# Four loads of 256 columns for each broadcast row in a four-layer graph attention kernel

## Chip, core and metric

The kernel runs on one core of a Trainium2 chip. The metric is the device time of one execution in microseconds (us). The time before is 2668.85 us, the median of three runs (2665.5 to 2671.96). The kernel is compiled as one straight program of 132436 instructions (a general path stands behind a branch at its end and is not taken with these inputs).

## The reference, cut to what matters

Sixteen graphs of 1024 nodes with 256 features pass through four layers. Each layer normalises, applies a ReLU, and adds a graph attention to its input:

```python
h = jnp.maximum(_layernorm(x, axis=-1), 0.0)
x = x + attention(h, adj, W, a_src, a_dst)        # four layers, the third with bias, ReLU, skip and layer norm per head
# inside, for a head:
e   = leaky_relu(s_src[:, :, None] + s_dst[:, None, :], slope)   # 1024 x 1024 for a graph and a head
e   = where(adj == 0, -inf, e)
out = softmax(e, axis=-1) @ (h @ W)
```

The first three layers have four heads of 64 columns, the last has one head of 256. All values are float32.

## The kernel before, in words

A softmax numerator of a head is a product of factors, so that for each block of 128 source nodes (a *tile*) one VectorE instruction makes 128 x 1024 numerators `p` from three things: the row `r`, which holds one value for each of the 1024 destination nodes and is the same in all partitions; a factor `fac` for each source node; and the mask. TensorE then multiplies the numerators (as weights, in pieces of 128 x 64) with the values `v`, 65 columns wide, and sums over the eight tiles of a head. A head has eight tiles, a unit (one layer of one graph) four heads, and 48 units of that kind are worked through in the order `ORDER`; the fourth layers of the graphs run beside them.

The row `r` comes to all partitions in four steps, in `prepare`:

- TensorE turns the values, VectorE copies them into the tile `row`.
- Two DMAs of the sync queue (SP) write them to DRAM, tensor `line`.
- For each head one DMA of the sync queue reads the head's 1024 values back to all 128 partitions (a source whose partition step is 0) into the tile `over`: named `rows` for the layers with four heads, of which there is one buffer (`ROWS = 1`), and `rows_one` for the last layer, also one buffer.
- ScalarE copies `rows` into one of two wide PSUM banks, `r` (`spread_row`), from which VectorE reads for eight tiles. `last_layer` copies quarters of `rows_one` in the same way.

As there is one `rows` buffer, the next row's load waits until ScalarE has copied the one before. The function `taken` says so to the planner, and the DMA waits for ScalarE's semaphore.

The order of all instructions is settled when the program is built. A planner (class `Plan`) keeps a clock for each engine. Each job is a generator that yields the engine it wants next and the earliest time; the loop at the end takes the step with the earliest planned time `when`, and the instructions go out in that order, each into its engine's queue. `plan.spend` moves an engine's clock; `plan.cost` has the costs, 400 ns of SP for a DMA. The queue of SP holds, besides the row loads: the loads of `x_cur` (128 KB each, eight for a graph), the transposed loads `mask` from `near`, the stores of `y` to `out_dram`, and the writes of `line`. SP takes them strictly in order, and a DMA that must wait for a semaphore holds up all behind it. The masks' source `near` is filled by casting DMAs that GpSimd issues.

PE's instructions are fetched by DMA while the program runs: the profile lists these transfers as a queue of their own, of the kind "instruction".

In the profile nearly every instruction has line 515, the line of the planner's helper that passes on each call (517 in the changed kernel, where the piece loads have lines of their own). Groups are therefore told apart by their tiles.

Of the kernel before, what the change touches and what calls it, by code (L numbers as in the profile page):

```python
# [20 lines left out]
P = 128  # L21
# [400 lines left out]
SPREAD = 0  # L422
SOONER = 300.0
AT_ONCE = -(10**6)
ACT_STATS = (0,)
SETTLE = 83.0
SECOND = 4000.0
# [109 lines left out]
def fast_path(  # L537
# [21 lines left out]
    nc = tc.nc  # L559
    ctx.enter_context(tc.manual_schedule())  # L560
    plan = Plan()
    pe, act, dve, pool, sp = (
        plan.engine(e, name)
        for e, name in (
            (nc.tensor, "PE"),
            (nc.scalar, "ACT"),
            (nc.vector, "DVE"),
            (nc.gpsimd, "POOL"),
            (nc.sync, "SP"),
        )  # L570
    )
    G, N, F = x.shape
# [82 lines left out]
    def bank():  # L655
        k = min(free_banks(), key=lambda k: banks[k])
        banks[k] = None
        if k >= BANKS:
            spare[0] += 1
            return ps_o.tile([P, 512], F32, name="po"), k  # L660
        return ps_p.tile([P, 512], F32, name=f"pp{k}"), k

    def drop(k: int):
        banks[k] = plan.now
# [17 lines left out]
    def wide_bank(dt=F32):  # L682
        k = wide_free.index(min(t for t in wide_free if t is not None))
        wide_free[k] = None
        return ps_r.tile([P, 4096 // mybir.dt.size(dt)], dt, name=f"r{k}"), k

    def leave_wide(k: int):
        wide_free[k] = plan.now
# [3 lines left out]
    def weights(layer: int):  # L692
# [43 lines left out]
        for k in range(KC):  # L736
            for c in range(KC):
                to = c * KC + k
                pe.transpose(pw[:, to * P : (to + 1) * P], given[:, k, c * P : (c + 1) * P], ident)
        yield "ACT", None, AT_ONCE  # L740
        if n == 1:
# [4 lines left out]
        drop(at)  # L746
        yield "PE", free_bank, AT_ONCE + 1
        pa, at = bank()
        for k in range(KC):
            for half in range(0, P, P // 2):  # L750
                for c in range(KC):
# [6 lines left out]
                    )  # L758
        yield "ACT", None, AT_ONCE
        act.copy(wa[layer][:, :, :, w : w + 2], pa[:, : KC * 2 * n].rearrange("p (k h c) -> p k h c", k=KC, h=n))  # L760
# [116 lines left out]
    def normal(es: list, rs: bass.AP):  # L877
# [25 lines left out]
        for e in es:  # L903
            yield "ACT", None, AT_ONCE
            e.hT = work.tile([P, KC, 2 * P], F32, name="hT", bufs=PAIRS)
# [5 lines left out]
    def project(e, i: int):  # L911
# [16 lines left out]
        e.read = plan.now  # L928
        yield "ACT", None, AT_ONCE
        act.copy(u.v[:, 2 * e.pair + i, :width], pv[:, :width])  # L930
# [18 lines left out]
    def prepare(u: "Unit"):  # L949
# [3 lines left out]
        width = n * (w + 2)  # L953
        by_act = layer in ACT_STATS and u.g.b >= BY_ACT and (layer < 3 or u.g.b < G - 2)
        yield "ACT" if by_act else "DVE", lambda: (
# [14 lines left out]
        if by_act:  # L970
            for i in range(2 * NB):
# [6 lines left out]
                b, c = i % NB, i // NB  # L978
# [48 lines left out]
        turned(pm, mine[:, 1, :])  # L1027
        yield "DVE", None, AT_ONCE
        top = small.tile([P, 1], F32, name="top", bufs=3)
# [16 lines left out]
        c = small.tile([P, 4, MAXN], F32, name="c", bufs=2)  # L1046
# [35 lines left out]
        if direct:  # L1082
# [20 lines left out]
            else:  # L1103
                yield "DVE", None, AT_ONCE
                over = units.tile([P, N], F32, name="rows_one", bufs=1)
# [16 lines left out]
        flat = line[: n * NB]  # L1122
        for h in range(len(u.row), n):
            yield "SP", lambda: (u.before is None or len(u.before.ps) == u.before.many * NB) if n == 1 else taken(ROWS, 4 * u.turn + h)
            if n > 1:
                over = units.tile([P, N], F32, name="rows", bufs=ROWS)
            else:
                over = units.tile([P, N], F32, name="rows_one", bufs=1)
            sp.dma_start(over, bass.AP(tensor=flat.tensor, offset=flat.offset + h * N, ap=[[0, P], [1, N]]))
            u.row.append((over, plan.now))  # L1130
        if n == 1:
            add(u.until + LATE, last_layer(u), plan.now)

    def turned(to, of):

        for half in range(0, P, P // 2):
            pe.matmul(to[half : half + P // 2, : P // 2], of, ident[:, half : half + P // 2])

    def taken(count: int, k: int):

        k -= count
        return k < 0 or main[k // H].weighed > k % H
# [59 lines left out]
    def row_due():  # L1202

        if rowed[0] == len(main) * H or rowed[0] * NB - at_tile[0] > ROW_LEAD or not free_wide():
            return False
        u, h = main[rowed[0] // H], rowed[0] % H
        return len(u.row) > h and max(u.row[h][1], free_wide())

    def spread_row():

        u, h = main[rowed[0] // H], rowed[0] % H
        rowed[0] += 1
        r, k = wide_bank()
        act.copy(r, u.row[h][0])
        u.across[h] = r, k, plan.now
        u.weighed += 1
# [179 lines left out]
    def last_layer(u: "Unit"):  # L1396

        due = lambda: (
            u.ready
            and hasattr(u, "flat")  # L1400
            and at_tile[0] >= u.gate
            and not row_due()
            and (late[0] < LATE_TILES or (at_tile[0] == len(tiles) and room() is not None and late[0] < TILES - 1))
        )
        free = lambda: due() and free_wide() and max(u.g.loaded, u.ready, free_wide())
        soon = lambda: u.ready and at_tile[0] == len(tiles) and room() and late[0] < TILES - 1 and max(u.ready, room())
        begun = at_tile[0]
        part = N // u.many
        for i in range(u.many):
            if i == 1:  # L1410
                add(u.until + LATE_SUMS, last_sums(u), plan.now)
            for j in range(0, NB, u.many):
                if u.kept:
                    yield "DVE", soon
                    late[0] += 1
                    cover_late(u, i, j, u.kept[0][:, i * part : (i + 1) * part])
                    continue
                yield "ACT", free, begun + LATE + int((i * NB + j) * SPREAD)
                late[0] += 1
                r, at = wide_bank()  # L1420
                act.copy(r[:, :part], u.row[0][0][:, i * part : (i + 1) * part])
                yield "DVE", room, at_tile[0]
                cover_late(u, i, j, r[:, :part])
                leave_wide(at)
        if u.kept:
            leave_wide(u.kept[1])
# [157 lines left out]
    def add(until, gen, ready, first=None):  # L1584
        jobs.append([until, ready, *(first or next(gen))[:2], gen])
# [3 lines left out]
    while True:  # L1589
        while begins and (begins[0][0] <= at_tile[0] or not jobs):  # L1590
            _, gen, until = begins.pop(0)
            add(until, gen, 0.0)
        can = []

        def offer(engine, ready, until, what):
            can.append((max(plan.free[engine], ready), until, engine, what))

        if row_due():
            offer("ACT", row_due(), at_tile[0], "row")
        if at_tile[0] < len(tiles) and room() is not None:  # L1600
            u, h, j = tiles[at_tile[0]]
            if h in u.across and u.g.loaded and u.ready:
                offer("DVE", max(u.across[h][-1], u.g.at[j % NQ2], u.ready, room()), at_tile[0] + SLACK, "cover")
        first = reach()
        if first:
            offer("PE", first[0], at_tile[0] + SLACK, "gather")
        for job in jobs:
            ready = job[3] is None or job[3]()
            if ready:
                ready = max(job[1], ready)  # L1610
                engine = job[2]
                offer(engine, ready, job[0], job)
        if not can:
            assert not jobs and not begins and at_tile[0] == len(tiles), "nothing can go on"
            break
        best = {}
        for e in ("SP", "POOL", "DVE", "ACT", "PE"):
            mine = [c for c in can if c[2] == e]
            if mine:
                first = min(c[0] for c in mine)  # L1620
                best[e] = min((c for c in mine if c[0] <= first + NEAR), key=lambda c: c[1])
        when, _, engine, what = min(best.values(), key=lambda c: c[0])
        plan.now, plan.last = when, None
        if what == "row":
            spread_row()
        elif what == "cover":
            cover(*tiles[at_tile[0]])
            at_tile[0] += 1
        elif what == "gather":
            gather()  # L1630
        else:
            step = next(what[4], None)
            if step is None:
                jobs.remove(what)
            else:
                wait = 0.0 if step[0] == engine else MARGIN.get(step[0], 40.0) if at_tile[0] < len(tiles) else 40.0
                what[0] = step[2] if len(step) > 2 else what[0]
                what[1:4] = [(when if step[0] == engine else plan.now) + wait, *step[:2]]


    nc.vector.tensor_scalar(bad[:, 2:3], greatest[:, G * LAYERS - 1 :], 1.0 / LEAST, bad[:, 3:4], ALU.is_le, ALU.is_lt)  # L1641
# [47 lines left out]
```

## Time and profile before

| | before |
|---|---|
| median of three runs | 2668.85 us |
| the profiled execution's own time | 2667.53 us |
| its span, first to last instruction | 2665.8 us |
| granted TensorE clock | 0.997 |
| PE busy | 2578.2 us (97%) |
| VectorE (DVE) busy | 2342.0 us (88%) |
| GpSimd (POOL) busy | 1890.4 us (71%) |
| ScalarE (ACT) busy | 1272.3 us (48%) |
| DMA queue of the sync and scalar engines, share of 16 DMA engines | 20.7% |
| DMA queue of GpSimd | 10.3% |
| instruction queue q8 | 467 packets, 7.65 MB, 1.2% |
| row loads | 190 of `rows` and 13 of `rows_one`, 512 KB each |

The span is what the profiler sees between the first and the last instruction; 1.7 us of the execution's time lie outside it. PE means TensorE's matmuls and PEld its weight loads, which overlap them. "Idle before" is an engine's idle time just before an instruction, with what released it; "issue" means that nothing which the profile shows was waited for. SP has no busy time: its instructions only wait and issue.

### The profile page before, as it was taken

To read this page: it belongs to the slowest core of one execution; us is meant where nothing else is said; L and a number is where in the kernel's file an instruction comes from. 1 tells how busy PE (TensorE), PEld (TensorE's weight loads), DVE (VectorE), ACT (ScalarE), POOL (GpSimd) and SP (SyncE) were. 2 spreads that over 40 slices of the span, in tenths; PEclk is the share of its full clock that TensorE was granted. 3 is DMA by queue.
4 is the path that set the end of the run, shared out by engine and by line. 5 is a ranking of instruction groups with operands and counts; after the bars stand their busy time and mean duration, and the time that the engine had idled before them with its cause. 6 is when DMAs were issued, how large, how long until landed. Compare 5 with 4: busy or idle time off the path is not lost. (4 is left out here: it accounts for less than half of the span.)

```text
span 2665.8 us, 132436 instructions
## 1 busy us (share of the span) xinstructions
PE 2578.2 (97%) x59354; PEld 2207.9 (83%) x59354; DVE 2342.0 (88%) x3723; ACT 1272.3 (48%) x3378; POOL 1890.4 (71%) x3375
## 2 busy tenths in 40 slices
PE   9999999999999999999999999999999999899998
PEld 7888887787988788889888788988778798888775
DVE  6799998897999797889998897999888699998984
ACT  4633563654346456533564644356364553443441
POOL 5556888765778877747887875688787565977761
PEclk9999999999999999999999999999999999999999
DMA  8533233443132253313314441323334441111100
GB/s 133 84 75 73 59 69 69 76 87 71 64 66 63 63 85 82 76 57 77 72 55 82 88 72 59 83 50 75 74 74 79 83 85 57 53 47 55 40 23 32
DMA packets 211122, 184.44 MB, mean 69 GB/s; under 512 B 150640, under 2 KB 184560, under 8 KB 210544
## 3 DMA queue, kind: packets, MB, share of 16 engines
q1 hardware_dynamic: 143088, 159.10, 20.7%
q0 software_dynamic: 67456, 16.78, 10.3%
q8 instruction: 467, 7.65, 1.2%
q14 instruction: 111, 0.91, 0.1%
HBM read 191.77 MB, written 34.39 MB: 85 GB/s over the span
## 5 line engine op out<-in xcount | busy, mean ns | idle before, releaser
L515 DVE SCALAR_TENSOR_TENSOR p<-r,fac,mask 128x1024 f32<-128x1024 f32 (+2 forms) x2032 | 2075.7, 1079 | 159.8 <-PE pp L515 80.8
L515 PE MATMUL po<-v,p 128*64 128x65 f32 x32992 | 1060.9, 224 | 36.4 <-issue 15.8
L515 PEld LDWEIGHTS po<-v,p 128*64 128x64 f32 x32992 | 1021.5, 138 | 87.9 <-issue 30.8
L515 PEld LDWEIGHTS po<-v_flat,p 128*64 128x64 f32 x16384 | 507.8, 138 | 56.8 <-issue 24.4
L515 PE MATMUL po<-v_flat,p 128*64 128x65 f32 x16384 | 525.0, 223 | 29.4 <-issue 14.7
L515 PE MATMUL pp<-wa,hT 128*64 128x264 f32 (+1 forms) x4032 | 474.2, 385 | 0.1
L515 PE MATMUL pp<-v_one,p 128*64 128x257 f32 x3584 | 403.6, 380 | 3.2 <-ACT y L515 2.9
L515 PEld LDWEIGHTS pp<-wa,hT 128*64 128x64 f32 x4032 | 278.4, 137 | 132.1 <-ACT v L515 0.4
L515 PEld LDWEIGHTS pp<-v_one,p 128*64 128x64 f32 x3584 | 248.6, 136 | 128.0 <-ACT y L515 4.6
L515 POOL TENSOR_SCALAR hn<-x_cur,rs 128x256 f32<-128x256 f32 x504 | 274.6, 558 | 33.3 <-PE pp L515 29.3
L515 POOL TENSOR_TENSOR att<-att,inv 128x512 f32<-128x512 f32 x128 | 133.7, 1045 | 221.2 <-DVE inv L515 207.7
L515 ACT COPY att<-po 128x260 f32<-128x260 f32 x256 | 96.2, 376 | 377.1 <-PE po L515 353.1
L515 ACT COPY v<-pp 128x264 f32<-128x264 f32 (+1 forms) x392 | 148.5, 379 | 215.0 <-PE pp L515 213.8
L515 POOL TENSOR_TENSOR x_cur<-att,x_cur 128x512 f32<-128x512 f32 x190 | 225.8, 1188 | 14.9
L515 ACT COPY r<-rows 128x1024 f32<-128x1024 f32 x190 | 194.0, 1021 | 21.8 <-DVE p L515 15.5
L515 ACT ACTIVATE att<-att,s 128x64 f32<-128x64 f32 x512 | 190.9, 439 | 23.3 <-POOL s L515 23.0
L515 ACT ACTIVATE hT<-pp 128x512 f32<-128x512 f32 x250 | 136.4, 598 | 128.1 <-PE pp L515 127.4
L515 ACT ACTIVATE att<-po,inv 128x64 f32<-128x64 f32 x512 | 118.7, 321 | 145.6 <-DVE inv L515 143.6
L515 POOL TENSOR_TENSOR y<-y,x_cur 128x256 f32<-128x256 f32 x116 | 84.3, 732 | 131.6 <-ACT y L515 112.1
L515 POOL TENSOR_TENSOR v<-v,fac 128x512 f32<-128x512 f32 x131 | 136.2, 1064 | 11.5 <-ACT fac L515 11.4
L515 DVE BATCH_NORM_STATS2 st<-x_cur 128x6 f32<-128x256 f32 x400 | 138.3, 411 | 3.3 <-DMA x_cur<-in_x_dram 2.9
L515 PE MATMUL pp<-ident,hn 128*128 128x128 f32 x1000 | 137.0, 280 | 0.2 <-DVE row L515 0.2
(124 smaller groups left out, 2150.0 us busy)
## 6 DMA issues: line engine op xcount, KB each, us to landing
rows<-line SPq DMA_DIRECT2D x190, 512.0 KB
out_dram<-y SPq DMA_DIRECT2D x128, 128.0 KB
x_cur<-in_x_dram SPq DMA_DIRECT2D x112, 128.0 KB
near<-in_adj_dram POOLq DMA_DIRECT2D x112, 128.0 KB, 4.3
rows_one<-line SPq DMA_DIRECT2D x13, 512.0 KB
x_cur<-in_x_dram SPq DMA_DIRECT2D x4, 512.0 KB
line<-row SPq DMA_DIRECT2D x96, 8.0 KB
block<-in_adj_dram POOLq DMA_DIRECT2D x4, 256.0 KB, 10.4
```

What stands on the lines that cost most here:

```text
L515: r = call(*a, **k)
```

## The change

The load of a row becomes `PIECES = 4` loads of 256 columns each. The first is issued where the whole load stood. The other three go into a list, `pieces`, each with the SP clock of that moment. One of them is issued after each later planner step of SP, if it was in the list before that step; a piece whose time is more than `ROW_APART` = 2500 ns of planned time before the next step of any engine is issued at once; and before ScalarE's copy of a row all that are left are issued. The planner's clock is charged once, for the whole row as before, and the pieces are issued past the planner. So the order of the instructions on PE, DVE, ACT and POOL is the same in both kernels, and only the sync queue differs: 203 loads become 812.

```diff
+PIECES = 4
+ROW_APART = 2500.0
...
@@ prepare
                 over = units.tile([P, N], F32, name="rows_one", bufs=1)
-            sp.dma_start(over, bass.AP(tensor=flat.tensor, offset=flat.offset + h * N, ap=[[0, P], [1, N]]))
+            of = lambda c, size: bass.AP(
+                tensor=flat.tensor, offset=flat.offset + h * N + c, ap=[[0, P], [1, size]]
+            )
+            plan.spend("SP", *plan.cost("SP", "dma_start", (over, of(0, N)), {}), [flat.tensor.name])
+            size = N // PIECES
+            nc.sync.dma_start(over[:, :size], of(0, size))
+            for c in range(size, N, size):
+                pieces.append((plan.free["SP"], over[:, c : c + size], of(c, size)))
             u.row.append((over, plan.now))
...
+    pieces = []
+    def next_piece():
+        nc.sync.dma_start(*pieces.pop(0)[1:])
+    def all_pieces():
+        while pieces:
+            next_piece()
...
@@ spread_row, and the same in last_layer
         r, k = wide_bank()
+        all_pieces()
         act.copy(r, u.row[h][0])
...
@@ the planner's loop
         when, _, engine, what = min(best.values(), key=lambda c: c[0])
         plan.now, plan.last = when, None
+        while pieces and pieces[0][0] + ROW_APART < when:
+            next_piece()
+        waiting = len(pieces)
         if what == "row":
             spread_row()
...
+        if engine == "SP" and waiting:
+            next_piece()
```

In the built program 175 of the 203 rows have their four loads directly behind one another in the sync queue. In 28 something stands between them: a row of the other kind (8), a store of `y` (8), a load of `x_cur` (11), and three mask transposes (the row issued at 64.8 us).

More of the change, by code (lines that the diff above doesn't have):

```diff
@@ L1420, in last_layer @@
                 r, at = wide_bank()
+                all_pieces()
                 act.copy(r[:, :part], u.row[0][0][:, i * part : (i + 1) * part])
```

## The prediction

> **What bounds the kernel now.** I read the busy times first, then what PE waits for, then the moments of those waits in the timeline and the DMA window.
>
> ```profile
> PE 2578.2 (97%) x59354; PEld 2207.9 (83%) x59354; DVE 2342.0 (88%) x3723; ACT 1272.3 (48%) x3378; POOL 1890.4 (71%) x3375
> ```
>
> PE is the bound. Its idle time is 2665.8 - 2578.2 = 87.6 us, and a change that adds or removes no work of PE can win at most that. The waits of PE, longest total first (us in total, times, longest):
>
> ```profile
> PE po L515 <- issue: 30.5, 32, 2.6
> PE po L515 <- ACT att L515: 15.8, 16, 1.4
> PE po L515 <- DVE p L515: 9.4, 9, 2.7
> ```
>
> The largest is "issue": PE waits for nothing that the profile shows. With two more of 0.5 us there are 34 such waits, 30.9 us. The view of all waits has what the row loads hold up directly:
>
> ```profile
> DVE p L515 <- ACT r L515: 32.7, 8, 10.4
> ...
> ACT r L515 <- DMA rows<-line: 3.1, 2, 2.1
> ```
>
> ScalarE waits for a row's landing twice, 3.1 us in all. So a row that lands earlier wins nothing; the question is what the loads do to other traffic. The timeline from 1056 to 1066 us shows one "issue" wait:
>
> ```profile
> 1055.78 7.27 PE L515 MATMUL po<-v,p 128*64 128x65 f32 x241
> 1058.73 7.60 SPq L515 DMA_DIRECT2D rows<-line  x2
> 1064.30 1.92 PE L515 MATMUL po<-v,p 128*64 128x65 f32 x56 [1.24 <-issue]
> ```
>
> and the DMA window 1059 to 1064 us (40 slices of 0.125 us, busy tenths) shows what the DMA engines did:
>
> ```profile
> DMA  0000062897799999032424160000000000000000
> ...
> q1 hardware_dynamic: 144, 0.52, 32.2%
> q8 instruction: 1, 0.02, 1.2%
> ```
>
> A row load, issued at 1058.73, moves packets from 1059.70 to 1062.12 us. The one instruction packet of this window begins at 1061.98, when the row is nearly through, and takes 0.93 us; PE starts again at 1064.30. Nothing else moves after the row, and PE starves for 1.24 us. I read this as a fetch that stood behind the row's packets.
>
> The packet records of the trace bear it out. Each of the 34 waits ends 2.2 to 2.9 us after an instruction packet began. In 17 of them (16.6 us) a row load was moving when that packet began, or had ended within 0.5 us before. In 8 (9.5 us) a row load stood shortly before or after it, mixed with GpSimd's adjacency packets. In 9 (4.8 us) there was no row load.
>
> How late a fetch begins can be read too. I count PE's instructions at each fetch's start, and take the 15th percentile of its 21 neighbours as punctual. The 90 fetches that fall due while a row load moves begin 1.31 us late on the mean, and 35 of them over 1.5 us late. The 228 due with no other traffic: 0.46 us, 17. The 22 due while packets of 1024 bytes move (`x_cur` and `out_dram`: 128 KB per load, the size and shape of the new pieces): 0.44 us, 3.
>
> **The change part by part.**
>
> *Packet work.* A row is now 128 packets of 4096 bytes, 199 ns each on the mean. The four pieces make 512 packets of 1024 bytes, which in the `x_cur` and `out_dram` transfers take 49 ns: 4 x 49 = 196 ns. The load on the DMA engines stays the same. Per engine a whole row is a run of 8 x 199 = 1.6 us; a piece is 8 x 49 = 0.39 us.
>
> *Fetches.* The nearest row for four loads in a train is the eight loads of `x_cur` in the queue of SP:
>
> ```profile
> 727.53 0.34 SPq L515 DMA_DIRECT2D rows<-line  x1
> 727.91 3.97 SPq L515 DMA_DIRECT2D x_cur<-in_x_dram  x8
> ```
>
> Their last packet lands at 735.05 us. After the row ahead of them has drained they take 4.95 us, 0.62 us a load, and need the engines for 0.39 us of it. A train of pieces thus leaves gaps in which a fetch can start. If late starts fall from 35 of 90 to the rate of the 1024-byte loads, 3 of 22, the share (35/90 - 3/22)/(35/90) = 0.65 of the starvation goes. On the 17 clear waits that is 16.6 x 0.65 = 10.8 us; on the 8 mixed ones, where adjacency packets (unchanged, lateness 1.08 us) do part, I take half the share: 9.5 x 0.33 = 3.1 us. Sum 13.9 us. The ends are 0 and 26.1 us (all 25 waits gone).
>
> *What is late next.* PE then meets its other waits sooner, for `att` (15.8 us) and `p` (9.4 us) above all. DVE is busy for 88% of the span, so it can follow a faster PE nearly everywhere. I let four fifths through, an estimate from that 88% rounded down: 13.9 x 0.8 = 11.1 us.
>
> [...]
>
> *Issue and landing.* SP issues 609 loads more. A follower starts 0.37 us (`x_cur` behind `rows`) to 0.475 us (`x_cur` behind `x_cur`) after the one before: 225 to 290 us of SP, spread over queues that mostly stand and wait. For a row the last piece is issued 1.1 to 1.4 us later than the whole load was. The whole load lands 3.44 us after its issue (median), its first packet at 0.97 us. Four pieces at the train's 0.62 us land at 0.97 + 4 x 0.62 = 3.45 us: no change, and I take that. From below, by issue and packets alone, it is 1.1 + 0.97 + 0.39 = 2.5 us, sooner; from above 3.44 + 1.1 = 4.5 us. The copies of `rows` have a median of 6.2 us between landing and start, and 10 of 190 have under 1.5 us. 1.1 us more would move those ten copies by 7.4 us in total (less a 0.4 us semaphore floor, the smallest distance seen). The copy then waits for four semaphores instead of one; they are long met for the rest, and ACT is busy for 48% only.
>
> *Between the pieces.* A store or an `x_cur` load between pieces (19 rows) costs one or two issues, under 1 us in nearly all, and these copies have 2.8 us or more to spare: nothing. The eight rows whose trains mix with the other kind cost 0.4 us where 0.8 is left: nothing. One row, issued at 64.8 us, has three mask transposes between its pieces; its copy starts 0.38 us after landing, and the third transpose starts 4.3 us after the row. Its last piece lands about 3 us later than now, in the warm-up. I charge 1 us of it, with ends 0 and 3.
>
> [...]
>
> **The sum.** 11.1 - 1.0 = 10.1 us less. The profiled execution has 2667.53 us, so it gives 2657.4; the median is 1.3 us above that execution, so I predict 2668.85 - 10.1 = 2658.8, rounded to 2659 us.
>
> **Rivals.**
>
> *The fetch still waits, so nothing moves.* 175 of 203 rows have their four pieces directly behind one another, so the change mostly does not put them "behind the next instruction". If a fetch must wait for all that stands in an engine's queue, four pieces are the same 1.6 us as one row, and the starvation stays. For it: the same bytes follow each other at 0.37 us, as fast as an engine needs for a piece (0.39 us). Against it: the 22 fetches among the 1024-byte loads. Time: 2668.85 less at most 2 us, 2668.
>
> *Rows land late, slower.* If the pieces' landing slips by more than 1.5 us (slow descriptor making, four semaphores, SP's queue), the ten tight copies are late, then VectorE's tiles (its wait for `r` grows from 32.7 us), then PE. It decides from a slip of about 2 us: the sum over the copies is then 17.2 us against 7.4 at 1.1 us, and half of it, with fetches unchanged, gives 2668.85 + 8.6 = 2677 us. For it: the eight `x_cur` loads behind a row land up to 4 us after their last issue. Against it: a good part of that is the row ahead in the same queue, and twelve tile buffers stand between VectorE and PE.
>
> *All row-linked starvation goes.* 2668.85 - 26.1 = 2643 us, if PE loses nothing of it elsewhere.
>
> **How the numbers follow.** The forecast with its upper rival gets 0.68, nothing moves 0.17, late rows 0.15. A measurement of this kernel can tell about 0.2%, 5.3 us, from no change. Of the forecast's 0.68 I put 0.04 within that bound, since 3 late starts of 22 is a thin base; of the second case's 0.17, 0.11 within it and 0.03 on each side. So faster 0.67, same 0.15, slower 0.18. The range reaches from 2646 (most of the 26 us) to 2673 (into late rows, half a per cent above the forecast); about one in ten is left out on each side. The forecast's own range is 2646 to 2665.
>
> **What would show it.** Right: PE's "issue" waits fall from 30.5 us to between 14 and 20; q8 still has 467 packets; q1 has about 78000 packets more at the same share, 20 to 21%; ScalarE's wait for row DMAs stays under 6 us; PE's busy time stays within 3 us of 2578. Wrong: "issue" waits of 25 us or more (the fetch waits for the whole train), or "ACT r <- DMA rows" of tens of us with the wait of `p` for `r` grown (late rows).

## The result and the profile after

The changed kernel is slower. Its median is 2681.47 us (2675.66 to 2688.42, nine runs) against 2667.55 us (2662.92 to 2671.96, nine runs) of the kernel before on the same chips; the ratio is 1.0053, 95% interval 1.0043 to 1.0063. The prediction was 2659 us, faster.

The page of the profiled execution (2681.47 us, its span 2679.7):

```profile
span 2679.7 us, 133512 instructions
...
PE 2588.9 (97%) x59354; PEld 2217.1 (83%) x59354; DVE 2343.1 (87%) x3723; ACT 1271.5 (47%) x3378; POOL 1885.8 (70%) x3375
...
q1 hardware_dynamic: 230784, 159.14, 23.1%
...
q8 instruction: 467, 7.65, 1.1%
```

The span is 13.9 us longer. PE still bounds the kernel, and both parts of its time grew: idle time from 87.6 to 2679.7 - 2588.9 = 90.8 us, busy time by 10.7 us for the same 59354 matmuls. The packets rose by 87696 (77952 of data and 16 more of 4 bytes for each of the 609 further loads), the bytes by next to nothing, and the share of the queue went from 20.7% to 23.1%. What PE waited for:

```profile
PE po L517 <- issue: 35.5, 49, 2.0
PE po L517 <- ACT att L517: 17.3, 17, 3.1
PE po L517 <- DVE p L517: 10.1, 11, 2.7
```

"Issue" was to fall to between 14 and 20 us. It rose from 31.0 us in 34 waits to 35.5 in 49. From the view of all waits, the two lines on the row's own path:

```profile
DVE p L517 <- ACT r L517: 39.6, 9, 10.4
...
ACT r L517 <- DMA rows<-line: 24.2, 16, 9.6
```

ScalarE waited for rows eight times as long as before (3.1 us). So both signs that the prediction named for "wrong" are there, and the experiments had to say which of them costs.

The DMA window from 1066 to 1072 us shows one row in its four pieces (40 slices of 0.15 us):

```profile
DMA  0000000822244677669444432354544443214000
...
rows<-line SPq DMA_DIRECT2D x4, 128.0 KB
```

The whole row of the prediction's window took 2.4 us from its first packet to its last. The packets of this one run from 1067.19 to 1071.54 us, 4.35 us, with the engines mostly at a third to two thirds, and the next instruction packet begins at 1071.54. Over all rows with no other transfer of the sync queue near them, the last packet comes 4.74 us after the first issue (median of 93), before it was 3.36 us (81). A row keeps each engine 1.83 us instead of 1.53.

About half of PE's further busy time, 5.1 of 10.7 us by the estimate below, came through its clock. The profile's windows around one long "issue" wait (columns: stretch, length, busy time and instructions of PE, PEld, DVE, ACT and POOL, granted clock, DMA share, GB/s):

```profile
975.20:978.60 3.40, 1.35 (x46) 1.22 (x44) 3.40 (x5) 3.21 (x13) 3.40 (x5) 1.00 0.25 72
978.60:982.00 3.40, 3.40 (x71) 3.40 (x68) 1.70 (x2) 0.60 (x2) 3.10 (x5) 0.50 0.91 143
```

After a stretch of 3.4 us in which PE was busy for only 1.35 us, the clock is half for the next 3.4 us. The kernel before has three such stretches up to 2640 us, the changed one six. Half of the three further ones is an estimate of what they cost: 3 x 3.4 / 2 = 5.1 us. One of the three more is chance: it follows a wait of 2.77 us for `p` (ending at 2602.2 us) that the kernel before has too (at 2587.8 us), without half clock behind it. With the 3.2 us of idle time that is 8.3 of the 13.9 us; the other 5.6 us are busy time that no view explains (pauses too short to be listed as waits would look so, but that is not shown).

The warm-up has its own piece. The timeline of SP from 63 to 82 us (start, duration, line, what is issued):

```profile
63.95 0.34 SPq L1136 DMA_DIRECT2D rows<-line  x1
64.47 1.19 SPq L517 DMA_TRANSPOSE mask<-near  x1
65.70 0.58 SPq L1147 DMA_DIRECT2D rows<-line  x1
66.33 2.55 SPq L517 DMA_TRANSPOSE mask<-near  x1
...
70.75 0.58 SPq L1147 DMA_DIRECT2D rows<-line  x1
```

And of the timeline of all engines there the copy of this row and the matmuls that waited:

```profile
77.42 1.02 ACT L517 COPY r<-rows 128x1024 f32<-128x1024 f32 x1 [9.60 <-DMA rows<-line]
...
81.06 2.22 PE L517 MATMUL po<-v,p 128*64 128x65 f32 x36 [3.10 <-ACT att L517]
```

The last piece of the third row is issued 6.8 us after the first. The copy starts at 77.42 us, before it was 69.21, PE then stands for 3.1 us, and its clock is half from 80.9 us for 3.4 us. Between 60 and 90 us of the span the changed kernel falls 4.2 us further behind.

### The profile page after: what moved, and what is told of

Read it like the earlier page. It is cut to its first block, busy times and chain, and to the rows that moved or that the text cites. A ratio compares the mean times of both kernels' runs of the same rounds, so it can differ in the third digit from the quotient of the medians.

```text
span 2679.7 us, 133512 instructions
## 1 busy us (share of the span) xinstructions
PE 2588.9 (97%) x59354; PEld 2217.1 (83%) x59354; DVE 2343.1 (87%) x3723; ACT 1271.5 (47%) x3378; POOL 1885.8 (70%) x3375
## 3 DMA queue, kind: packets, MB, share of 16 engines
q1 hardware_dynamic: 230784, 159.14, 23.1%
## 5 line engine op out<-in xcount | busy, mean ns | idle before, releaser
L517 ACT COPY r<-rows 128x1024 f32<-128x1024 f32 x190 | 194.0, 1021 | 39.8 <-DMA rows<-line 24.2
```

The costliest lines, as they stand in the source:

```text
L517: r = call(*a, **k)
```

## The experiments

All are built on the kernel before unless said otherwise. But for the one named below, PE, DVE, ACT and POOL have the same instructions in the same order as before. "Issue" is PE's issue waits, "row wait" ScalarE's wait for row loads of both kinds, "late" the fetches (of 458) that begin over 1.5 us late, counted as in the prediction (how "punctual" is taken moves these by a few). The last three are read from one execution each, which can lie off the median: 2675.96 us for "64 columns, gap, 960 columns" with a median of 2681.63, 2695.25 for "8 x 16 partitions" with 2686.99.

| row load | ratio to before | 95% interval | issue us | row wait us | late |
|---|---|---|---|---|---|
| before: one load | 1 | | 31.0 | 3.9 | 87 |
| changed: 4 x 256 columns, spread | 1.0053 | 1.0043 to 1.0063 | 35.5 | 24.2 | 118 |
| 4 x 256 columns together | 1.0038 | 1.0025 to 1.0051 | 38.4 | 18.4 | 109 |
| 2 x 512 columns together | 1.0025 | 1.0011 to 1.0039 | 29.6 | 7.3 | 101 |
| 2 x 512 columns with a gap | 0.9996 | 0.9987 to 1.0005 | 27.0 | 7.1 | 91 |
| 64 columns, gap, 960 columns | 1.0052 | 1.0039 to 1.0064 | 36.9 | 14.7 | 116 |
| one load, and 512 bytes to 128 partitions | 1.0040 | 1.0027 to 1.0053 | 38.4 | 5.1 | 114 |
| 16 partitions, gap, 112 partitions | 0.9988 | 0.9976 to 1.0000 | 24.0 | 16.3 | 87 |
| 2 x 64 partitions | 0.9998 | 0.9989 to 1.0006 | 27.4 | 16.3 | 93 |
| 2 x 64 partitions with a gap | 0.9983 | 0.9972 to 0.9993 | 20.5 | 21.5 | 84 |
| 4 x 32 partitions together | 0.9932 | 0.9918 to 0.9946 | 15.7 | 15.6 | 54 |
| 4 x 32 partitions, spread as in the change | 0.9949 | 0.9936 to 0.9962 | 12.5 | 17.6 | 53 |
| 8 x 16 partitions | 1.0076 | 1.0059 to 1.0094 | 11.4 | 92.0 | 59 |
| one load in bfloat16 | 0.9950 | 0.9937 to 0.9964 | 18.2 | 1.9 | 77 |

**Column pieces, nothing between them.** In `prepare`, in place of the one load (`of` and the planner's charge as in the change):

```diff
+            for c in range(0, N, N // 4):
+                nc.sync.dma_start(over[:, c : c + N // 4], of(c, N // 4))
```

> The four column loads of each row stand directly behind one another in the sync queue, none behind another instruction. Theory A (the train of four loads keeps the DMA engines longer than one load, 3.8 us against 2.4 us from its first to its last packet, so that more instruction fetches start late and PE starves): as slow as the changed kernel, 2677 to 2686 us, PE's issue waits 34 to 40 us. Theory B (rows land about 1.4 us later, the copies wait, then VectorE, then PE): also 2677 to 2686. Theory C (what stands between the pieces of 28 rows, the three transposes in the warm-up above all, is the cost): back to 2666 to 2671 us.

2678.58 us, and 38.4 us of issue waits. So theory C, what stands between the pieces, is not the main cost. The two intervals, 1.0025 to 1.0051 here and 1.0043 to 1.0063 for the change, overlap; but this kernel gains no lag worth naming between 60 and 90 us (0.5 us against 4.2), so some of what lies between them is the row in the warm-up.

**The row late, its bytes together.** A load of 64 columns, two loads of one value into another tile `late_to`, then 960 columns:

```diff
+            nc.sync.dma_start(over[:, :64], of(0, 64))
+            for c in range(2):
+                nc.sync.dma_start(late_to[:1, c : c + 1], <one value of line>)
+            nc.sync.dma_start(over[:, 64:], of(64, N - 64))
```

> Each row in a load of 64 columns, two single values to another place, and then one load of 960 columns: the large load starts about 1.1 us later than in the kernel before, as the last piece does, but its packets stay large and together. Theory A: the time from first to last large packet stays at 2.4 us, so 2667 to 2672 us and issue waits near 31 us. Theory B: ScalarE waits for rows for 15 to 25 us, and the time is 2675 to 2682 us. Theory C: 2667 to 2670.

2681.63 us, as B said. But the issue waits went to 36.9 us, which B does not explain: the small load of 64 columns had done something by itself. So this run could not decide, and two others took its parts apart.

**The small load alone.** The whole row as before, and behind it one load that brings 4 bytes to each partition of `late_to`:

> The kernel before, and behind each whole row load one more load that brings one value (4 bytes) to each of the 128 partitions of another tile: 512 bytes, which nobody reads. Theory D (a load from DRAM to 128 partitions keeps instruction fetches from starting for about 1.5 us, whatever its bytes; loads to fewer partitions let them in between): fetches held up for about 1 us longer per row, PE's issue waits 34 to 42 us, 2673 to 2682 us. Theory A (time on the DMA engines, in bytes): the extra load is 8 packets of 10 ns on each engine, so 2666 to 2670 us and 31 us. Theory B (late rows): the row lands as before, so 2666 to 2670.

2675.28 us: 0.4% slower for 512 bytes that nobody reads. From the view of all waits in this kernel:

```profile
PE po L515 <- issue: 37.4, 48, 2.3
...
ACT r L515 <- DMA rows<-line: 3.7, 4, 2.0
...
PE pp L515 <- issue: 1.0, 2, 0.5
```

The rows land as before, and PE starves as in the changed kernel. The packet records show it too: between 1.25 and 3.25 us after the issue of a row 16 fetches begin, in the kernel before 44, and in the next 0.75 us 76, before 47. So fetches wait for the small load as well. This is the cause shown by itself: one more load from DRAM to 128 partitions per row can cost as much as three (0.40% here, 0.38% with four column pieces together). It is no fixed price: two halves by columns (below) are one more such load too, with no more issue waits (29.6 us, before 31.0).

**The lateness alone.** 16 partitions, two single values, then the other 112 partitions, all with 1024 columns:

> Each row in a load of 16 partitions, two single values to another place, and one load of the other 112 partitions, all with 1024 columns: the large load starts about 1.1 us later than the whole row did, and no load to 128 partitions is added. Theory D: issue waits 26 to 33 us as with the whole row. What theory B (late rows) is worth at this slip is then seen alone: with B, 2673 to 2680 us; without it 2664 to 2670 us.

2661.49 us, ratio 0.9988. From the view of all waits:

```profile
PE po L515 <- issue: 24.0, 34, 2.3
...
ACT r L515 <- DMA rows<-line: 9.1, 9, 3.2
...
ACT r L515 <- DMA rows_one<-line: 7.2, 7, 1.5
```

ScalarE waited 16.3 us for rows, four times as long as before, and the kernel is not slower; VectorE's wait for `r` stayed at 32.7 us. The issue waits fell by 7.0 us, below D's range, so the lateness is not quite alone here. But the span of the profiled execution fell by 6.8 us with them, which leaves next to nothing for theory B at this slip.

**Cut by partitions.**

```diff
+            for c in range(0, P, P // 4):
+                nc.sync.dma_start(over[c : c + P // 4], <the row of 1024 to P // 4 partitions>)
```

> Each row in four loads of 32 partitions with all 1024 columns, directly behind one another: four issues as in the changed kernel, but packets of 4096 bytes, a quarter as many. If the length of the train comes from the number of loads (0.47 us apart at least, A by issue): landing near 4.5 us after the first issue and 2676 to 2684 us. If it comes from the number of packets (A by packets): landing 3.4 to 3.9 us, 2667 to 2673 us. Theory B goes with the landing: 2675 to 2682 if that is over 4.4 us.

Neither reading of theory A had this: 2650.49 us, 0.68% faster than before and 1.2% faster than the change, with the same four issues.

```profile
PE po L515 <- issue: 15.7, 23, 2.6
PE po L515 <- ACT att L515: 15.4, 16, 1.4
PE po L515 <- DVE p L515: 10.5, 9, 2.7
```

The starvation is halved, as the prediction had hoped of the columns. The issue waits fell by 15.3 us, the span of the profiled execution by 14.8 us (the medians by 18.1 us).

> Each row in two loads of 64 partitions with all 1024 columns. Theory D: between the whole row (2668) and four loads of 32 partitions (2650): 2655 to 2664 us, issue waits 20 to 28 us. If only the number of loads counted, as the late column pieces suggest: 2670 or more.

> Each row in eight loads of 16 partitions with all 1024 columns. Theory D: fetches are let in at least as well as with four, issue waits 10 to 17 us; but the last load is issued some 3 us after the first, so the row lands 1.5 to 2 us later than with four and ScalarE waits for it 30 us or more. Theory B prices that: 2655 to 2665 us. Without B: 2646 to 2653 us.

Two halves gained nothing (2666.23 us), which D had not expected. Eight pieces had the fewest issue waits of the table, 11.4 us, and were slower, 2686.99 us. Here rows come late enough to matter. From the view of all waits:

```profile
ACT r L515 <- DMA rows<-line: 72.4, 23, 10.0
...
DVE p L515 <- ACT r L515: 46.8, 20, 10.7
...
ACT y L515 <- DMA out_dram<-y: 30.5, 15, 3.4
```

The sync queue has 1624 row loads to issue, 0.46 us apart, so the eight of a row take about 3.6 us, and rows and stores come late (ScalarE's wait for stores was 8.0 us before). PE's waits for `att` and `p` rose from 15.8 and 9.4 us to 27.2 and 15.3. About half of the loss, 12.6 us, is there by 90 us, in the warm-up.

**The change with its pieces cut by partitions.** The changed kernel, `size = P // PIECES` and `over[c : c + size]` in place of columns, the pieces spread as in the change:

> The changed kernel with its pieces cut by partitions (four of 32 partitions with 1024 columns) in place of columns; each further piece behind the next instruction of the sync queue as in the change. Theory D: as fast as the four loads by partitions that stand together, 2647 to 2656 us, issue waits 13 to 18 us. If the place of the pieces in the queue is what costs (theory C): 2660 or more.

2650.95 us. So the place of the pieces in the queue does no harm by itself; what harms is how they are cut.

**Half the bytes.** Rows rounded to bfloat16 (`row`, `line`, `rows` and `rows_one` declared so), one load each. A first kernel let the planner price the smaller load, which moved instructions on all engines:

> The rows are rounded to bfloat16 on their way through DRAM (row, line, rows and rows_one in 2 bytes), one load a row as in the kernel before: half the bytes, packets of 2048 bytes. Theory A: the engines are held for about half as long, PE's issue waits fall from 31 us to 20 to 25 us, 2655 to 2662 us. Theory B: rows land about 0.7 us sooner, and there are only 3.1 us of waits to win: 2665 to 2669 us.

2713.3 us, ratio 1.0162, with issue waits of 12.4 us; because of the other order it says nothing on the loads. With the planner's price held:

> Rows rounded to bfloat16 on their way through DRAM, one load a row, and the planner's price of the loads held at that of the 4-byte row, so that the order of the instructions on the other engines is that of the kernel before. Theory D (128 partitions hold fetches up whatever the bytes): 2662 to 2668 us, issue waits 24 to 31 us. Theory A (bytes): 2648 to 2658 us, issue waits 14 to 20 us.

2652.32 us and 18.2 us of issue waits: theory A's range, not D's. So the bytes of a load count too, and D in its strict form ("whatever its bytes") is wrong.

> Each row in two loads of 512 columns to all 128 partitions, directly behind one another. Theory D: two such loads hold up fetches as the row with its 512 bytes behind it did (0.4% slower): 2673 to 2680 us, issue waits 34 to 40 us. Theory A (time on the DMA engines): packets of 2048 bytes cost little more than one of 4096, so 2667 to 2672 us.

2670.09 us and 29.6 us of issue waits: A's range, not D's. The ratio is above 1 all the same, but the profiled execution, 2668.5 us, is only 1 us longer than that of the kernel before, so its trace does not tell why.

**Loads apart.** Single values between the two loads, two of them between halves by partitions, three between halves by columns:

> Each row in two loads of 64 partitions as in the kernel with two such loads (0.9998 of before, issue waits 27.4 us), with two loads of a single value between them, which put the second half about 0.75 us later. Theory E (a fetch starts where the queue of loads runs dry): the first half is through before the second begins, issue waits 14 to 22 us, 2648 to 2658 us. Theory F (what counts is the number of packets that a load puts on each engine, four here): as without the gap, 25 to 30 us, 2662 to 2668 us.

> Each row in two loads of 512 columns to 128 partitions as in the kernel with two such loads (1.0025 of before, issue waits 28.6 us), with three loads of a single value between them, which put the second load about 1.1 us later. Theory E: issue waits 18 to 25 us, 2655 to 2664 us. Theory F: 27 to 33 us, 2667 to 2676 us.

The packet records show what E says. With the gap between halves by partitions, of the fetches 1 begins in the half microsecond from 1.5 to 2.0 us after the row's first issue, 33 from 2.25 to 2.75 us, 12 from 3.0 to 3.75 us, and 63 in the next 0.75 us: they are let in between the loads. The times follow only in part: 2663.63 us (issue waits 20.5, E's range, the time in F's) and 2665.74 us (issue waits 27.0, F's range, the time between E and F). The halves by columns are faster than without a gap (ratio 0.9996 against 1.0025); of those by partitions (0.9983 against 0.9998) the two intervals overlap.

**Two more steps by partitions.** `x_cur` in four loads of 32 partitions too:

> Rows in four loads of 32 partitions, and each load of x_cur (128 partitions of 256 columns, 1024-byte packets) in four loads of 32 partitions too. Theory D: of the 23 fetches that fall due within 2.2 us of an x_cur load in the kernel before, 18 are over 1.5 us late; with four loads they are let in, issue waits 1 to 4 us less than with the rows alone, 2645 to 2650 us. If the 448 further issues hold up the sync queue more than that: 2651 to 2656 us.

2682.05 us, ratio 1.0053. The issue waits did fall, to 11.4 us, but the eight loads of a graph are now 32 issues in a row (348 issues more, not the 448 of the expectation), with row loads behind them, and ScalarE's wait for `rows` is 72.8 us. The loss is in the warm-up: the kernel is 13.2 us behind at 90 us and 14.3 us at 2640 us, so this run does not tell what the cut of `x_cur` is worth later. And the first three rows whole, the others in four:

> Rows in four loads of 32 partitions, but the first three rows of the program in one load each, as in the kernel before. The kernel with all rows in four is 3.8 us behind the kernel before at 90 us of the span; if that is the row among the mask transposes, this one is 2 to 4 us faster than that kernel: 2645 to 2650 us, 0.9915 to 0.993 of before.

2649.23 us, ratio 0.9929 (0.9914 to 0.9943): the lag at 90 us fell from 3.8 to 1.3 us, and the median by 1.3 us, less than these runs can tell. It is the fastest version seen, beside the one without this step.

## Why the prediction was wrong

*That row loads starve PE through its instruction fetches* was right. Four loads by partitions halved the issue waits (31.0 to 15.7 us) and took 0.68% off; 512 bytes more per row put 0.40% on.

*The step that failed: that the 1024-byte loads stand for the pieces.* I took 22 fetches due while 1024-byte packets moved, 3 of them late, and gave that rate to the pieces. That group mixed two kinds. Counted by the issue before them, the 23 fetches due within 2.2 us of an `x_cur` load (DRAM to 128 partitions, the form of the pieces) begin 1.97 us late on the mean, 18 of them over 1.5 us. The 32 due within 2.2 us of a store to `out_dram`: 0.24 us, 1. I had the rows that spoke against the change, averaged a part of them with stores, and left the rest out, as only fetches were counted that fell due while nothing but such packets moved. The comparison is not a clean one of directions: the `x_cur` loads come in trains of up to eight (84 of the 116 are issued directly behind another one and within 2 us of it, 15 so behind a row load), and 13 of their fetches fell due while a row's packets moved too (12 late; of the other nine, five), while of the 128 stores 28 are issued so behind another one. The term of -11.1 us has the wrong sign; with nothing between the pieces the runs show about +10 us (0.38%).

*That trains leave gaps in which a fetch can start* was wrong for column pieces. Between 1.25 and 2.5 us after a row's first issue 7 fetches begin in the kernel before, 20 with four column pieces together, 44 with four pieces of 32 partitions. Why the two cuts differ is not shown. Both are issued 0.47 us apart, and a piece holds each engine for about as long, 8 packets x 58 ns = 0.46 us by columns and 2 x 218 ns = 0.44 us by partitions, so the time on the engines does not tell them apart; the number of packets does. But that alone is not it either: a row in bfloat16 has as many packets as before, half as large, and gains 0.5%. Halves of 64 partitions, 0.49 us apart with 4 x 0.22 = 0.88 us each, leave no gap by these numbers, and one made by hand cut the issue waits by a quarter (27.4 to 20.5 us). What in the DMA engines makes a fetch wait stays open.

*The packet work* was to stay as it was, 196 ns for 199; row packets of 1024 bytes took 58 ns and not the 49 of `x_cur` and `out_dram`, so a row keeps each engine 1.83 us and not 1.53.

*The landing* was 4.74 us, past even the upper end of 4.5. But its price, the rival "rows land late", was too high at this slip: 16.3 us of waits for rows cost nothing in the run that had them alone. At eight pieces, with 92.0 us of such waits, late rows do cost.

*The row between the transposes* was charged with 1 us, ends 0 and 3; about 4 us were lost by 90 us, as the copy started 8.2 us later and not 3, with a stretch at half clock behind it. The last piece was issued 6.8 us after the first and landed over 6 us after that, while the transposes' packets moved; that they held it up is likely but not shown.

*The rival "nothing moves"* was nearer to the runs. With four column pieces together 49 of 128 fetches that fell due while a row moved by itself began over 1.5 us late, against 23 of 229 with nothing moving; the prediction had counted 35 of 90 and 17 of 228 in the kernel before. In the changed kernel 23 fetches begin between 3.0 and 3.75 us after a row's first issue and 63 between 4.5 and 5.5 us, in the kernel before 54 and 38. But four pieces are not the same as one row, they are longer: their last packet comes 4.74 us after the first issue, that of the whole row after 3.36. *What I left out* is that a wait of PE of about 2 us can cost another 1.7 us through the clock (the clock was half for 3.4 us at four waits of 1.93 to 3.10 us, listed below; the 1.7 us are an estimate, half of 3.4). This is not the main cost: up to 2640 us the kernel with four column pieces together has three such stretches, as the kernel before, and the one with four pieces by partitions together has six, as the changed kernel.

The 609 more loads of the change cost 14 us by the medians; as many more by partitions came with 18.1 us less. In the kernel before 371 of the 458 fetches counted began at most 1.5 us late; of its 31.0 us of "issue" waits 15.3 us went by cutting the loads in another direction.

## What to carry to other kernels

Where the busiest engine waits for "issue", look which transfers were under way when its instruction packets began, and ask of each kind of load by itself how late the fetches behind it start; do not pool loads and stores by packet size. If a load to 128 partitions stands in the way, try to cut it by partitions, not by columns, and only so far as the issuing queue can follow: four pieces of 32 were faster by 0.7%, two of 64 no faster, eight of 16 slower by 0.8%. A row that is a microsecond later may cost nothing (16.3 us of ScalarE's waits at a ratio of 0.9988) while a load of 512 bytes for each row costs 0.4%.

## What the runs showed of the hardware that I had not expected

- A load of 4 bytes to each of 128 partitions behind each of 203 row loads made the kernel 8.8 us slower by the medians: 43 ns each.
- Behind stores of the same size and packets as the `x_cur` loads fetches were hardly late, 0.24 us on the mean against 1.97 us; but of the 116 loads 84 are issued directly behind another one and within 2 us of it, of the 128 stores 28.
- A broadcast row in 1024-byte packets costs an engine 1.83 us, in 4096-byte packets 1.53 us. In the same kernel `x_cur` and `out_dram` packets of 1024 bytes took 49 ns, row packets 58.
- After waits of PE of 3.10, 2.04 and 1.93 us (the changed kernel, ending at 81.1, 977.6 and 1468.8 us) and of 2.25 us (the kernel before, ending at 483.6 us) the clock was half within 1.5 us of the wait's end, for about 3.4 us. In the window shown PE had been busy for 40% of the stretch before. The stretches at half clock lie on a grid of 3.413 us: in five traces (before, changed, four column pieces together, four pieces by partitions together, 512 bytes more), up to 2640 us, each follows a stretch of that grid in which PE was busy for 44% or less, and none follows one with 46% or more. So the same wait of 2.77 us costs clock in one kernel and not in another.
